# Delta rule over 32 head pairs: the inverse may cross turns, and side work on VectorE is queued behind the recurrence's last result

## The chip, the cores and the metric

The kernel runs on one core of one Trainium2 chip. The metric is the device time of one execution in microseconds (us); times of several runs are given by their median. Five engines work side by side, each through its own queue: TensorE (PE: matrix products), VectorE (DVE), ScalarE (ACT), GpSimd (POOL) and SyncE (SP, which here only starts transfers).

## The reference

A decoder layer in three parts, all in float32: a gated delta rule, a quantised cross attention, and an attention block with a mixture of experts. The change is in the first part. For 4 sequences of 512 tokens and 16 heads of width 128 it computes, token after token,

```
q, k, v = causal convolution (4 taps) and SiLU of x @ W.T
q, k    = each divided by its norm
S_t     = g_t * S_(t-1) + k_t (beta_t * (v_t - g_t * S_(t-1)^T k_t))^T
o_t     = S_t^T q_t
out     = (o * rsqrt(mean(o * o) + eps) * norm_w * silu(x @ Wg.T)) @ Wo.T
```

S is a 128 x 128 state for each head. The mean runs over all 16 heads of a token.

## The kernel before

The recurrence is done in chunks of 128 tokens, 4 for each sequence. Inside a chunk the tokens depend on each other through a triangular matrix (`at`, from the products of the keys); its inverse turns the chunk into a few matrix products. From chunk to chunk goes only the state.

The work is cut into 32 pairs: two heads of one sequence (`HG = 2`, 8 pairs a sequence, 4 sequences). For each pair there are these steps, all written as Python generators that stop at each `yield`:

- `stage1(m)` (L530): convolutions of k and q, norms, decay factors, the triangular matrices. POOL computes powers for the norms there (L566 to L570, tiles `rk`, `ee`, `ke`, `nr`), once VectorE has clamped the sums (`ss`, L565). `at` goes to memory and comes back as 32 x 32 blocks (`iA`, L641).
- `stage2_inverse(m)` (L644): the inverse of the diagonal 32 x 32 blocks by elimination, 31 rows of two operations (L654 and L655, tiles `iW` and `iT`), each on the result of the row before. Even pairs do this on VectorE, odd pairs on POOL. Then the result is written to memory (`t_d`, L658), a transposed copy too (L659, L660), and both are read back in the layout of the matmuls (`T`, L663, and `X`, L665).
- `stage2_values(m)` (L670): convolutions of v and of the gate.
- `stage3(m)` (L700): four steps that extend the block inverse to 128 x 128 (its first matmuls, L714, read `T`), and then the recurrence, chunk by chunk: L766 multiplies keys and state, VectorE makes `r` of it (L768), L775 applies the inverse, ScalarE copies the result `u` (L777), L785 makes the addition to the state, VectorE the new `state` (L790), and L793 and L795 the output `po`. At the end VectorE reads `po` in `og` (L807) and in the squares (L811).
- `output(m)` (L821): the product with Wo (L840), added up over the 8 pairs in `xa` (L845). After a sequence's last pair the rms factor follows: `rsqrt` (L118 to L123, a power on POOL, tile `a_rs`) and L858.

In turn m (the loop at L938) `stage3(m)` is the main line. After each of its steps one round of the side work is traced: `output(m-1)`, `stage1(m+2)` (two steps a round), `stage2_values(m+1)`, `stage2_inverse(m+1)` (two steps a round) and, once a sequence, the `prologue` of the next sequence. What is left when `stage3` has ended is run out at the turn's end.

This program order is not the order on the engines. A scheduler takes for each engine the work that it expects to be ready, with the program order as priority, and may move an operation far ahead. `tc.issue_after(ins)` limits that: what is traced in its block on the engine of `ins` may not stand ahead of `ins` in that engine's queue (order only, no wait for the result). Before the change it is used for POOL alone: odd pairs' rows and the gate's products stand behind the latest norms (`norms_[-1]`, L653 and L798).

Of the kernel before, what the change touches and what calls it, by code (L numbers as in the profile page):

```python
# [33 lines left out]
ALU = mybir.AluOpType  # L34
# [13 lines left out]
VD = H1 * P  # L48
# [50 lines left out]
def decoder(ctx: ExitStack, tc: tile.TileContext, a: dict, out: bass.AP):  # L99
    nc = tc.nc  # L100
# [7 lines left out]
    mhalf = const.tile([P, 64], F32, name="mhalf")  # L108
# [9 lines left out]
    def rsqrt(dst, src, pool, add=0.0, mul=1.0):  # L118

        n = src.shape[1]  # L120
        t = pool.tile([P, 64], F32, name="rsq")
        nc.vector.tensor_scalar(t[:, :n], src, mul, add, ALU.mult, ALU.add)
        nc.gpsimd.tensor_tensor(dst, t[:, :n], mhalf[:, :n], ALU.pow)  # L123

    def layernorm(dst, src, pool):

# [42 lines left out]
    def idle(n):  # L169
        for _ in range(n):  # L170
            yield
# [154 lines left out]
    with ExitStack() as st:  # L326
# [4 lines left out]
        small = st.enter_context(tc.tile_pool(name="a_small", bufs=4))  # L331
# [198 lines left out]
        def stage1(m):  # L530
# [11 lines left out]
            ss = small.tile([P, HG * TB], F32, name="ss", bufs=2)  # L542
            for p in range(HG):
                t = live.tile([P, S], F32, name="kT")
# [3 lines left out]
            xnT, beta, gam, ngam, gend, gall = seqs[b]  # L548
            gb = rows(0)
            load_weights(m + 1, 1)  # L550
            for p in range(HG):
# [3 lines left out]
                t = s1.tile([P, TB, P], F32, name="ktok")  # L555
# [6 lines left out]
            rk, ee, ke = (small.tile([P, HG * TB], F32, name=n, bufs=2) for n in ("rk", "ee", "ke"))  # L562
            nr = small.tile([P, HG * TB], F32, name="nr", bufs=4)
# [3 lines left out]
            nc.gpsimd.tensor_tensor(ee, rk, rk, ALU.mult)  # L567
            nc.gpsimd.tensor_tensor(ee, ee, flat(beta), ALU.mult)
            nc.gpsimd.tensor_tensor(ke, ee, flat(gend), ALU.mult)
            norms_.append(nc.gpsimd.tensor_tensor(nr, ss, rk, ALU.mult).ins)  # L570
            em = []
            for p in range(HG):

# [5 lines left out]
            for p in range(HG):  # L579
                scale(em[p], em[p], ee, p)  # L580
                pk = p_b.tile([P, TB, P], F32, name="pb")
# [12 lines left out]
            for p in range(HG):  # L594
# [5 lines left out]
                t = w2.tile([P, S], F32, name="cv", bufs=5)  # L600
# [3 lines left out]
                pq = p_b.tile([P, TB, P], F32, name="pb")  # L604
# [3 lines left out]
                t = live.tile([P, TB, P], F32, name="pt", bufs=6)  # L608
# [16 lines left out]
            for p in range(HG):  # L625
                t = live.tile([P, TB, P], F32, name="kdec", bufs=4)
# [4 lines left out]
            nc.gpsimd.tensor_tensor(rq, rq, mhalf[:, 0 : HG * TB], ALU.pow)  # L631
            keys[m] = (kT, kd_, qg, pt, nr, rq)

        inverses, norms_ = {}, []

        def load_blocks(m, ats):

# [6 lines left out]
        def stage2_inverse(m):  # L644

            nb = HG * TB * 4
            A, T, W, ats = inverses.pop(m)
            eng = nc.vector if m % 2 == 0 else nc.gpsimd
            for i in range(31):
                n, w = 31 - i, i + 1  # L650
                u = W[:, : n * w].rearrange("p (a b) -> p a b", a=n)

                with tc.issue_after(norms_[-1]) if m % 2 and m > 1 else ExitStack():  # L653
                    eng.tensor_tensor(u, A[:, i, i + 1 :].unsqueeze(2).to_broadcast([nb, n, w]), T[:, i, :w].unsqueeze(1).to_broadcast([nb, n, w]), ALU.mult)  # L654
                    eng.tensor_tensor(T[:, i + 1 :, :w], T[:, i + 1 :, :w], u, ALU.add)  # L655
                yield
            dT, dX = inv_d[m % 2]
            nc.sync.dma_start(blocks(dT), T)  # L658
            eng.tensor_copy(A, T.rearrange("p t j -> p j t"))  # L659
            nc.sync.dma_start(blocks(dX), A)  # L660
            yield
            t = w2.tile([P, HG * TB, P], F32, name="T", bufs=1)
            nc.sync.dma_start(t, squares(dT))  # L663
            x = w2.tile([P, HG * TB, P], F32, name="X", bufs=2)
            nc.sync.dma_start(x, squares(dX))  # L665
            Ts, Xs = ([v[:, p * TB : (p + 1) * TB, :] for p in range(HG)] for v in (t, x))
            inverses[m] = (Ts, Xs, ats)
            yield

        def stage2_values(m):  # L670

# [28 lines left out]
        def stage3(m):  # L700
# [56 lines left out]
            for c in range(TB):  # L757
                cs = slice(c * P, (c + 1) * P)
                rs = []
                for p in range(HG):  # L760
                    h = hg * HG + p
                    if c == 0:
                        rs.append(v_[p][:, 0, :])
                        continue
                    pk = p_s.tile([P, P], F32, name="ps")
                    nc.tensor.matmul(pk, kT[p][:, cs], st_[p], start=True, stop=True)  # L766
                    r = small.tile([P, P], F32, name="r", bufs=3)
                    nc.vector.scalar_tensor_tensor(r, pk, ngam[:, h, c : c + 1], v_[p][:, c, :], ALU.mult, ALU.add)  # L768
                    rs.append(r)
                if c:  # L770
                    yield
                us = []
                for p in range(HG):
                    pu = p_s.tile([P, P], F32, name="ps")
                    nc.tensor.matmul(pu, Xs[p][:, c, :], rs[p], start=True, stop=True)  # L775
                    u = small.tile([P, P], F32, name="u", bufs=4)
                    nc.scalar.copy(u, pu)  # L777
                    us.append(u)
                yield
                nst = list(st_)  # L780
                for p in range(HG):
                    h = hg * HG + p
                    if c < TB - 1:
                        pn = p_s.tile([P, P], F32, name="ps")
                        nc.tensor.matmul(pn, kd_[p][:, c, :], us[p], start=True, stop=True)  # L785
                        s_ = small.tile([P, P], F32, name="state", bufs=4)
                        if c == 0:
                            nc.scalar.copy(s_, pn)
                        else:
                            nc.vector.scalar_tensor_tensor(s_, st_[p], gall[:, h, c : c + 1], pn, ALU.mult, ALU.add)  # L790
                        nst[p] = s_
                for p in range(HG):
                    nc.tensor.matmul(po[p][:, c, :], us[p], pt[p][:, c, :], start=True, stop=c == 0)  # L793
                    if c > 0:
                        nc.tensor.matmul(po[p][:, c, :], st_[p], qg[p][:, cs], start=False, stop=True)  # L795
                st_ = nst
                if 0 < c <= HG:
                    with tc.issue_after(norms_[-1]):  # L798
                        nc.gpsimd.tensor_tensor(gs[c - 1], gs[c - 1], rb[c - 1], ALU.mult)
                yield  # L800

# [19 lines left out]
        def output(m):  # L821


            b, hg = divmod(m, NHG)
            og = outs.pop(m)
            wot = w2.tile([P, HG, D], F32, name="wot", bufs=2)
            nc.sync.dma_start(wot, a["a_wo"][hg])
            xs = []

            def load(c):  # L830
                xs.append(w2.tile([P, D], F32, name="x_in", bufs=2))
                nc.sync.dma_start(xs[c], x_t[:, b * TB + c, :])

            if hg == NHG - 1:
                load(0)
                load(1)
            for c in range(TB):
                pw = p_b.tile([P, D], F32, name="pb")
                for p in range(HG):
                    nc.tensor.matmul(pw, og[p][:, c * P : (c + 1) * P], wot[:, p, :], start=p == 0, stop=p == HG - 1)  # L840
                if hg == 0:
                    xa[c] = w2.tile([P, D], F32, name="xa", bufs=4)
                    nc.vector.tensor_copy(xa[c], pw)
                else:
                    nc.vector.tensor_tensor(xa[c], pw, xa[c], ALU.add)  # L845
                yield
            if hg == NHG - 1:
                yield from idle(4)
                pq = p_b.tile([P, TB], F32, name="pb")
                for c in range(TB):  # L850
                    nc.tensor.matmul(pq[:, c : c + 1], acc[b][:, c * P : (c + 1) * P], ones1, start=True, stop=True)
                rs = small.tile([P, TB], F32, name="a_rs")
                yield
                rsqrt(rs, pq, small, add=1e-6, mul=1.0 / VD)
                yield
                for c in range(TB):
                    xr = xa[c]
                    nc.vector.scalar_tensor_tensor(xr, xr, rs[:, c : c + 1], xs[c], ALU.mult, ALU.add)  # L858
                    if c + 2 < TB:
                        load(c + 2)  # L860

                    (nc.gpsimd if m == NP - 1 else nc.sync).dma_start(x1d[b * TB + c], xr)
                    yield
# [72 lines left out]
        run(itertools.islice(pair0, 3 * HG + 1))  # L936
        run(turns((stage2_inverse(0), 2), (chain(pair0, turns((stage1(1), 2), (stage2_values(0), 1))), 1), (prepare(), 1)))
        for m in range(NP):  # L938
            rest = []
            if m == NP - 2:  # L940
                first.close()
                x_keep = top.enter_context(tc.tile_pool(name="x_keep", bufs=1, side="right", reuse_waits="tile"))
# [16 lines left out]
                rest.append((stage1(m + 2), 2))  # L959
            if m + 1 < NP:  # L960
                rest.append((stage2_values(m + 1), 1))
                rest.append((stage2_inverse(m + 1), 2))
            if (m + 4) % NHG == 0 and (m + 4) // NHG < B:
                rest.append((prologue((m + 4) // NHG), 1))
            rest = turns(*rest)
            for _ in stage3(m):
                next(rest, None)
            run(rest)
        run(turns((output(NP - 1), 1), (cross(1), 2)))

# [572 lines left out]
```

## Time and profile before

| what | value |
|---|---|
| median of 3 runs | 3871.29 us (3865.89 to 3873.21) |
| the profiled execution | 3873.35 us, its span on the core 3871.6 us |
| TensorE busy | 3445.1 us, 89% of the span |
| VectorE busy | 2243.0 us, 58% |
| ScalarE busy | 1568.5 us, 41% |
| POOL busy | 1379.5 us, 36% |
| mean granted TensorE clock | 0.942 |

The delta rule takes the first 56% of the span: the first L714 starts at 150.9 us, the last at 2114.4 us. The other two parts follow.

```profile
PE   5898999789987989897889789999999999898897
...
L655 POOL TENSOR_TENSOR iT<-iT,iW 32x31 f32<-32x31 f32 (+15 forms) x496 | 275.8, 556 | 38.9
L654 POOL TENSOR_TENSOR iW<-iA,iT 32x31 f32<-32x31 f32 (+15 forms) x496 | 268.6, 541 | 41.1 <-DMA iA<-at_d 2.4
...
L655 DVE TENSOR_TENSOR iT<-iT,iW 32x31 f32<-32x31 f32 (+15 forms) x496 | 211.9, 427 | 10.3
...
L654 DVE TENSOR_TENSOR iW<-iA,iT 32x31 f32<-32x31 f32 (+15 forms) x496 | 204.2, 412 | 10.7
...
L775 PE MATMUL ps<-r,X 128*128 128x128 f32 x384 | 81.4, 311 | 139.0 <-DVE r L768 138.4
```

The first line is TensorE's busy share in 40 equal slices of the span, in tenths. A group's line reads: line, engine, operation, output and inputs, count | busy us in all, mean ns of one | idle us of the engine just ahead of it, and what ended most of that. TensorE is busy nearly everywhere; where it is not, the question is what the next instruction in its queue waited for.

### The profile page before, as it was taken

The page shows a single profiled execution, that of the slowest core. Times are in us where ns is not written, and L with a number is a line of the kernel's source. Part 1 is how long each engine was busy: PE and PEld are TensorE (multiplying, and loading weights), DVE is VectorE, ACT ScalarE, POOL GpSimd, SP SyncE. Part 2 cuts the span into 40 slices and gives each one's busy share as a digit, 9 for nine tenths or more (in the row PEclk, how much of TensorE's full clock was granted, in tenths as well). Part 3 has the DMA queues.
Part 4 walks back from the last instruction along what each step waited for, and adds up shares of the span by engine and source line. Part 5 has one row for each costly group of instructions (what it writes and reads, how often), then busy time and mean ns, then how long its engine had stood idle before and what let it go on. Part 6 is the DMA issues. An engine that isn't in the chain of part 4 may idle for free. (4 is left out here: it accounts for less than half of the span.)

```text
span 3871.6 us, 48770 instructions
## 1 busy us (share of the span) xinstructions
PE 3445.1 (89%) x16466; PEld 1947.6 (50%) x16466; DVE 2243.0 (58%) x4923; ACT 1568.5 (41%) x4382; POOL 1379.5 (36%) x1941
## 2 busy tenths in 40 slices
PE   5898999789987989897889789999999999898897
PEld 3455555445554545454545445555555555454443
DVE  5477766666675667656764556655665565554111
ACT  3444444335443435343433334444444444343121
POOL 1425553455355444543455222113212221211442
PEclk8899999899998999998999899999999999999898
DMA  5333334333333334334333155445544444456444
GB/s 158 109 101 101 100 88 119 109 99 100 114 99 107 97 108 113 95 89 130 96 96 111 56 176 161 143 146 158 161 134 139 144 139 143 139 173 204 82 82 92
DMA packets 391880, 465.56 MB, mean 120 GB/s; under 512 B 128451, under 2 KB 242115, under 8 KB 391440
## 3 DMA queue, kind: packets, MB, share of 16 engines
q1 hardware_dynamic: 380080, 438.03, 38.0%
q0 software_dynamic: 10112, 21.58, 3.1%
q8 instruction: 132, 2.16, 0.2%
q10 hardware_dynamic: 1440, 2.84, 0.2%
q14 instruction: 116, 0.95, 0.1%
HBM read 401.76 MB, written 64.81 MB: 121 GB/s over the span
## 5 line engine op out<-in xcount | busy, mean ns | idle before, releaser
L511 PE MATMUL pb<-xnT,w 128*128 128x512 f32 x2048 | 972.5, 615 | 0.0
L511 PEld LDWEIGHTS pb<-xnT,w 128*128 128x128 f32 x2048 | 385.2, 198 | 429.9 <-issue 412.0
L522 DVE SCALAR_TENSOR_TENSOR cv<-pb,pp,cv 128x511 f32<-128x511 f32 (+2 forms) x576 | 427.1, 741 | 230.5 <-ACT cv L519 209.8
L1085 PE MATMUL pb<-c_q,hT 128*128 128x512 f32 x768 | 357.1, 603 | 10.6 <-DMA c_q<-in_c_wq_dram 6.0
L655 POOL TENSOR_TENSOR iT<-iT,iW 32x31 f32<-32x31 f32 (+15 forms) x496 | 275.8, 556 | 38.9
L654 POOL TENSOR_TENSOR iW<-iA,iT 32x31 f32<-32x31 f32 (+15 forms) x496 | 268.6, 541 | 41.1 <-DMA iA<-at_d 2.4
L519 ACT ACTIVATE cv<-pb,pp 128x512 f32<-128x512 f32 x192 | 148.2, 772 | 263.5 <-PE pb L511 263.5
L840 PE MATMUL pb<-wot,og 128*128 128x512 f32 x512 | 251.1, 613 | 0.0
L1191 PE MATMUL pw<-c_o,oT 128*128 128x512 f32 x512 | 240.7, 600 | 2.9 <-DVE oT L1183 2.9
L1085 PEld LDWEIGHTS pb<-c_q,hT 128*128 128x128 f32 x768 | 142.0, 193 | 166.3 <-issue 149.3
L655 DVE TENSOR_TENSOR iT<-iT,iW 32x31 f32<-32x31 f32 (+15 forms) x496 | 211.9, 427 | 10.3
L566 POOL TENSOR_TENSOR rk<-ss,mhalf 128x8 f32<-128x8 f32 x32 | 53.3, 1666 | 460.2 <-DVE ss L565 460.2
L1157 ACT ACTIVATE e<-pb,nm,rq 128x128 f32<-128x128 f32 (+3 forms) x256 | 157.0, 618 | 140.3 <-DVE nm L1155 108.7
L654 DVE TENSOR_TENSOR iW<-iA,iT 32x31 f32<-32x31 f32 (+15 forms) x496 | 204.2, 412 | 10.7
L775 PE MATMUL ps<-r,X 128*128 128x128 f32 x384 | 81.4, 311 | 139.0 <-DVE r L768 138.4
L274 POOL TENSOR_SCALAR x_e<-x_e 128x1024 f32<-128x1024 f32 x64 | 68.1, 1064 | 331.0 <-ACT x_e L269 241.2
L1181 PE MATMUL po<-eT,val 128*128 128x512 f32 x320 | 171.0, 628 | 6.8 <-ACT eT L1179 3.8
L598 POOL TENSOR_TENSOR qg<-qh,row 128x512 f32<-128x512 f32 x64 | 84.5, 1325 | 223.3 <-ACT qh L525 221.1
L1151 PE MATMUL pb<-kT,qT 128*128 128x256 f32 (+3 forms) x576 | 162.7, 409 | 0.8 <-ACT x_e L269 0.8
L269 ACT ACTIVATE x_e<-pb,nm 128x256 f32<-128x256 f32 x256 | 118.2, 477 | 102.4 <-DVE nm L266 102.4
L775 PEld LDWEIGHTS ps<-r,X 128*128 128x128 f32 x384 | 63.1, 204 | 171.1 <-DVE r L768 149.6
L1013 POOL TENSOR_TENSOR rope_s<-q,tab 128x128 f32<-128x128 f32 x64 | 35.2, 550 | 314.9 <-DVE q L1115 269.3
(330 smaller groups left out, 6629.1 us busy)
## 6 DMA issues: line engine op xcount, KB each, us to landing
c_o<-in_c_wo_dram SPq DMA_DIRECT2D x128, 512.0 KB, 4.2
c_q<-in_c_wq_dram SPq DMA_DIRECT2D x128, 512.0 KB, 4.6
w<-in_a_w_dram SPq DMA_DIRECT2D x124, 512.0 KB, 4.2
row<-g_d SPq DMA_DIRECT2D x64, 512.0 KB, 5.0
at_d<-at SPq DMA_DIRECT2D x64, 256.0 KB, 2.2
T<-t_d SPq DMA_DIRECT2D x32, 512.0 KB, 6.1
X<-x_d SPq DMA_DIRECT2D x32, 512.0 KB, 6.6
rrow<-r_d SPq DMA_DIRECT2D x32, 512.0 KB, 3.8
```

The costliest lines, as they stand in the source:

```text
L511: nc.tensor.matmul(pj, wt[:, kd, p * P : (p + 1) * P], xnT[:, kd, :], start=kd == 0, stop=kd == KD - 1)
L519: nc.scalar.activation(ac, pj, AF.Identity, bias=cb[:, m, h : h + 1], scale=cw[:, m, h, 3:4])
L522: nc.vector.scalar_tensor_tensor(ac[:, j:], pj[:, : S - j], cw[:, m, h, 3 - j : 4 - j], ac[:, j:], ALU.mult, ALU.add)
L654: eng.tensor_tensor(u, A[:, i, i + 1 :].unsqueeze(2).to_broadcast([nb, n, w]), T[:, i, :w].unsqueeze(1).to_broadcast([nb, n, w]), ALU.mult)
L655: eng.tensor_tensor(T[:, i + 1 :, :w], T[:, i + 1 :, :w], u, ALU.add)
L775: nc.tensor.matmul(pu, Xs[p][:, c, :], rs[p], start=True, stop=True)
L840: nc.tensor.matmul(pw, og[p][:, c * P : (c + 1) * P], wot[:, p, :], start=p == 0, stop=p == HG - 1)
L1085: nc.tensor.matmul(pj, hT[:, kd, :], w[:, kd % 2, :], start=kd == 0, stop=kd == KD - 1)
L1151: nc.tensor.matmul(ps[:, m, k * P : (k + w) * P], qT[g][:, n + m, :], kT[:, g, j : j + w, :], start=True, stop=True)
L1157: nc.scalar.activation(e[n + m][:, :nk], ps[:, m, :nk], AF.Exp, bias=nm[:, n + m : n + m + 1], scale=rq, accum_out=es[:, n + m : n + m + 1])
L1181: nc.tensor.matmul(po, val[:, g, :], eT, start=k == 0, stop=k == c)
L1191: nc.tensor.matmul(pw, oT[:, h + m, :], w[:, m, :], start=g == 0 and h + m == 0, stop=g == 3 and h + m == 3)
```

## The change

A new generator `inversions` takes the place of `stage2_inverse(m + 1)` in the side work: it first finishes the inverse of pair m+1, and then, from step 10 of the turn's 15 on, may begin that of pair m+2 and hand it over in `begun`. Every round of side work is traced behind `vital[-1]`, the latest `r` or `state` that VectorE makes for the recurrence. `norms_` becomes `factors`, to which the rms factor of a sequence's end also belongs; pair 1 is tied to it too. Four idle rounds in `output` become two and two.

```diff
-        nc.gpsimd.tensor_tensor(dst, t[:, :n], mhalf[:, :n], ALU.pow)
+        return nc.gpsimd.tensor_tensor(dst, t[:, :n], mhalf[:, :n], ALU.pow).ins
...
-            norms_.append(nc.gpsimd.tensor_tensor(nr, ss, rk, ALU.mult).ins)
+            factors.append(nc.gpsimd.tensor_tensor(nr, ss, rk, ALU.mult).ins)
...
-        inverses, norms_ = {}, []
+        inverses, begun, vital, factors = {}, {}, [], []
...
-                with tc.issue_after(norms_[-1]) if m % 2 and m > 1 else ExitStack():
+                with tc.issue_after(factors[-1]) if m % 2 else ExitStack():
...
+        def inversions(m, step, turn):
+
+            if m + 1 < NP:
+                yield from begun.pop(m + 1) if m + 1 in begun else stage2_inverse(m + 1)
+            if m + 2 < NP:
+                while turn and (turn[0] < step or m + 2 not in inverses):
+                    yield
+                begun[m + 2] = stage2_inverse(m + 2)
+                while turn:
+                    next(begun[m + 2])
+                    yield
...
-                    nc.vector.scalar_tensor_tensor(r, pk, ngam[:, h, c : c + 1], v_[p][:, c, :], ALU.mult, ALU.add)
+                    vital.append(nc.vector.scalar_tensor_tensor(r, pk, ngam[:, h, c : c + 1], v_[p][:, c, :], ALU.mult, ALU.add).ins)
...
-                            nc.vector.scalar_tensor_tensor(s_, st_[p], gall[:, h, c : c + 1], pn, ALU.mult, ALU.add)
+                            vital.append(nc.vector.scalar_tensor_tensor(s_, st_[p], gall[:, h, c : c + 1], pn, ALU.mult, ALU.add).ins)
...
-                    with tc.issue_after(norms_[-1]):
+                    with tc.issue_after(factors[-1]):
...
-                yield from idle(4)
+                yield from idle(2)
...
-                rsqrt(rs, pq, small, add=1e-6, mul=1.0 / VD)
+                factors.append(rsqrt(rs, pq, small, add=1e-6, mul=1.0 / VD))
                 yield
                 for c in range(TB):
+                    if c == 2:
+                        yield from idle(2)
...
-            rest = []
+            rest, turn = [], [0]
...
-                rest.append((stage2_inverse(m + 1), 2))
+                rest.append((inversions(m, 10, turn), 2))
...
             for _ in stage3(m):
-                next(rest, None)
+                with tc.issue_after(vital[-1]) if vital else ExitStack():
+                    next(rest, None)
+                turn[0] += 1
+            turn.clear()
             run(rest)
```

## The prediction

> **What bounds the kernel now.** First the busy table and its stretches: TensorE is busy 1762 of the 2000 us between 165 and 2165, the 32 turns of the delta rule, and nothing in the diff acts after them. So at most some 240 us of TensorE idleness is at stake. Then the waits of TensorE in that stretch (us in total, times, longest):
>
> ```profile
> PE ps L775 <- DVE r L768: 138.4, 50, 13.1
> PE pb L714 <- DMA T<-t_d: 40.4, 8, 6.2
> PE ps L766 <- DVE state L790: 15.5, 9, 7.4
> ```
>
> Two causes: the recurrence's result `r` comes late from VectorE, and a pair's inverse `T` comes late from memory. L714 is the first work of a turn. Its starts in the timeline divide the turns: odd turns take 58.0 us on average (15 of them, 1 to 29), even ones 68.2, those with a prologue (4, 12, 20) 73.2, those with a sequence's end (8, 16, 24) 78.1. Turns 14 and 15 by stretch (PE, PEld, DVE, ACT, POOL busy):
>
> ```profile
> 1044.24:1112.78 68.54, 55.02 (x298) 31.84 (x297) 48.24 (x82) 26.88 (x78) 39.25 (x56) 0.94 0.29 76
> 1112.78:1171.29 58.51, 56.38 (x297) 32.00 (x297) 35.78 (x73) 25.56 (x76) 22.16 (x33) 0.95 0.40 112
> ```
>
> TensorE has 55 to 56 us of work in either. Turn 14's timelines of PE, POOL and SP, in that order, show where the rest goes:
>
> ```profile
> 1098.02 0.80 PE L775 MATMUL ps<-r,X 128*128 128x128 f32 x2 [5.40 <-DVE r L768]
> ...
> 1106.17 0.39 PE L795 MATMUL po<-qg,state 128*128 128x128 f32 x2
> ...
> 1112.78 0.26 PE L714 MATMUL pb<-T,at 128*32 128x32 f32 x1 [6.22 <-DMA T<-t_d]
> ```
>
> ```profile
> 1069.49 1.65 POOL L566 TENSOR_TENSOR rk<-ss,mhalf 128x8 f32<-128x8 f32 x1 [18.89 <-DVE ss L565]
> ...
> 1102.80 0.30 POOL L655 TENSOR_TENSOR iT<-iT,iW 32x31 f32<-32x31 f32 x1
> ```
>
> ```profile
> 1103.12 0.31 SPq L658 DMA_DIRECT2D t_d<-iT  x1
> ...
> 1106.25 0.46 SPq L663 DMA_DIRECT2D T<-t_d  x1
> ```
>
> See in it: the odd pair's inverse runs on POOL. From `rk` (25.25 us into the turn) to the write of `t_d` are 33.6 us, from there to L714 9.7. That chain ends the turn; without the 5.4 us stall TensorE would have waited 11.6 at L714. The even pair's inverse, on VectorE, is done in the middle of the odd turn (its last row at 1137.6, needed at 1171.3), so no even turn waits for its `T`.
>
> **What the Trainium skill says.** "PSUM — Partial Sum Buffer", section Engine vs sequencer instructions: the queues of ScalarE, VectorE and GpSimd are strict FIFO and matmuls start in program order. The trace agrees: L714 has 6.22 us of idle TensorE ahead of it though the convolution behind it (L511) needs nothing of `T`. "TensorE: Matmul & The Clock Gate", section What's actually happening: after an idle window of some 3.4 us the array runs at half clock for about as long. Agreed: the first twelve L511 records of a turn take 8.02 us after the 6.22 us wait and 5.42 in turn 14, which had none. "SBUF — State Buffer", section SBUF: two separate sides: VectorE with two SBUF inputs and GpSimd exclude each other on a shared port. Agreed: the elimination's VectorE rows take 0.6 to 0.7 us beside POOL's and 0.3 to 0.4 alone.
>
> **The change, part by part.** No arithmetic is added or removed; only order.
>
> 1. *The early start.* An inverse takes 33 yields (31 rows and two), the generator is advanced twice a round, so it ends in round 17. A turn has 15 yields of stage3 (4 for the solve, 2 for chunk 0, 3 each for the others). So in round 15 it stands at row 29; `turn.clear()` comes before the rest is run out, and the begun inverse then finds `turn` empty and takes no step. Each turn thus hands nothing on. The early start never happens: worth 0.
>
> 2. *VectorE work queued behind `vital[-1]`.* Rows of the even pair were floated by the scheduler into idle time of the turn before. Now row 2k or 2k+1 may not stand ahead of the recurrence result of its round. In the built program's order, turn 15 to 16 on VectorE ends
>
> ```
> L768 r x2 (chunk 3)
> rows 24 to 29 of pair 16, between them L575 em x2
> L807 og x2, L811 cv x2
> row 30 of pair 16, L659 copy
> ```
>
> and this holds for every even pair from 2 to 30: row 30 stands behind `og`, which waits for the turn's last L795. TensorE's order still has L714 directly behind L795. So in odd turns L714 must now wait for og, cv, row 30, the write of `t_d` and the read of `T`.
>
> Odd turn, from its L714, taking turn 15's offsets (it too follows a wait, so it starts cold): `r` of chunk 1 at 28.5 as before. Rows now between the results delay `state` by 1 us and the chunk-2 `r` to 43.3; the new TensorE order puts 4 us of other matmuls there, so I count 2 us of stall where before were 1.5+0.35. Chunk-3 `r` is done at 55.5, L795 at 59. VectorE still has two scans (1.2 each), 12 row operations (6 us beside POOL, 3 alone; I take 4.4 with the gaps): og starts at 62.3, og and cv take 1.41+1.28, row 30 0.4: 65.4. SP's queue has the `rq`, `r_d` and `rrow` transfers ahead of L658; by the same trace they pass at about 66. Write to landing 2.3 (list of transfers), issue of the read to L714 6.5 (1106.25 to 1112.78): 66+2.3+0.1+6.5 = 75, against 58: +17. Floor: L795 ends at 57, og at once, 57+2.7+0.4+2.3+0.1+6.5 = 69. Ceiling, if all rows run at the shared-port price and stalls add up to 4 us: 80.
>
> Even turn: the POOL order behind `rk` is the same (1 row operation, gs, 1, gs, 40), so the stall at L775 that goes turns into a longer wait at L714. The turn now begins cold, `rk` at 27.7 (as turns 3, 7, 11 after a wait: 27.5 to 28.0): 27.7+33.6+9.7, less 0.6 because a weight load moved behind the read of `T`: 70.4, +2.2. What is late next is nothing: TensorE arrives at about 60.
>
> 3. *Sequence ends (turns 8, 16, 24).* `rsqrt` moves ahead, and POOL's rows wait for it, so L858 no longer waits 19.5 us for POOL's `a_rs`, and the stalls of 13.1 and 6.5 us go. But then POOL's chain with the extra power (0.6) ends the turn: 71 instead of 78.1.
>
> 4. *Small ones.* Pair 1 (odd) is now tied to `factors` too: turn 0 becomes 27.0+33.6+9.1 = 70 instead of 59.5. Three fewer table loads on ScalarE, hidden under TensorE. Prologue turns have 8 us more matmuls, which cover POOL's chain: 72 instead of 73.2. Turn 30 starts cold: +2.
>
> Sum: 15 odd turns x 17 = +255; 8 plain even turns (2, 6, 10, 14, 18, 22, 26, 28) x 2.2 = +18; prologue 3 x -1 = -3; ends 3 x -7 = -21; turn 0 +10; turn 30 +2: +261. The profiled execution took 3873.35 (span 3871.6), the median of the runs is 2 less: 3871+261 = 4132.
>
> **Rivals.**
>
> *The floor.* As forecast, but VectorE reaches og when L795 ends: 69 to 70.5 in odd turns, +165 to +188 in them, with the rest some 4050. For it: VectorE is busy only 36 of 58 us in turn 15. Against: some rows that stood in turn 14 are now in turn 15, and two scans stand behind the last `r`.
>
> *VectorE becomes the bound.* Odd turns of 80 and more: at least 4210. For it: 45 row operations at up to 0.65 us, and PSUM is held until VectorE has evacuated. Against: POOL works on rows in parallel only in parts of the odd turn.
>
> *The stalls go and nothing takes their place* (faster). Place: L775 in odd turns and turns 8, 16, 24. If row 30 were out before og, L714 of even turns would find its `T`, and 15 x 1.5 + 3 x 7 = 43 us would be saved: 3830. It decides from the point where row 30 and the write come some 12 us ahead of L795. If the early start also took effect for the POOL pairs, all three waits above would go: 3871-194 = 3677. Against: the order of the built program, the same in all 15 odd turns.
>
> **How the numbers follow.** Forecast (odd turns of 70.5 to 79.5) 0.82; floor 0.07; VectorE bound 0.07; nothing in their place 0.03; the two effects cancelling 0.01. A measurement of this kernel can tell about 0.2% from no change. Range: 15 x -4.5 from 4132 is about 4065, 15 x +4 with 5 more in the even turns about 4195; this leaves out little more than the two neighbours. Faster 0.03, same 0.01, slower 0.96.
>
> **What would show it.** Right: L714 waits for `T` in nearly every turn, some 15 us at the start of even turns and 9 to 11 at that of odd ones, together about 370 us; the wait of L775 for `r` falls from 138 to under 50; the copy L659 on VectorE comes behind L811; L858's wait for `a_rs` is gone; odd turns near 75, plain even ones near 70. Wrong: an even turn that begins without a wait for `T` (then row 30 was out in time), or L775's wait still above 100 us (then VectorE, not the inverse, is the bound).

## The result, and the profile after

The changed kernel takes 4069.87 us (median of 4 runs, 4068.42 to 4075.21), the kernel before 3870.56 us in the same comparison (4 runs, 3865.89 to 3873.21). The ratio is 1.0519, interval 1.0501 to 1.0537: 5.2% slower. The profiled execution took 4070.2 us, its span 4068.4 us.

The page's table of busy time and its line of TensorE by slices:

```profile
PE 3452.6 (85%) x16466; PEld 1942.1 (48%) x16466; DVE 2273.2 (56%) x4923; ACT 1572.8 (39%) x4379; POOL 1390.2 (34%) x1941
...
PE   5878787877978787887878788999999999899797
```

TensorE has the same work (3445.1 us before); its share falls, and only in the slices of the delta rule. Its mean granted clock fell from 0.942 to 0.924, but its busy time rose by only 7.5 us, so the loss is nearly all waiting, not slower matmuls. The last turn starts at 2310.8 us instead of 2114.4: the 196 us that were lost lie in the turns. TensorE's waits in that stretch, in the changed kernel (us in total, times, longest; the lines of code have moved by 12: L714 is L726, L766 is L778, L775 is L787):

```profile
PE pb L726 <- DMA T<-t_d: 325.2, 29, 15.1
PE pb L607 <- ACT qh L525: 47.9, 15, 3.2
PE ps L787 <- DVE r L780: 28.2, 16, 3.1
PE ps L778 <- DVE state L802: 10.5, 15, 0.7
```

The wait for `r`, 138 us before, has shrunk to 28; the wait for `T` has grown from 40 to 325 us, and comes in 29 turns instead of 8. One thing was late, now another is, and by more. The lengths of the turns (from one start of L714 or L726 to the next, in us):

| turns | before | predicted | after |
|---|---|---|---|
| odd, 1 to 29 (mean of 15) | 58.0 | 75 | 73.7 |
| plain even (mean of 8) | 68.2 | 70.4 | 66.7 |
| with a prologue (4, 12, 20) | 73.2 | 72 | 67.6 |
| with a sequence's end (8, 16, 24) | 78.1 | 71 | 72.9 |
| 0 | 59.5 | 70 | 62.8 |
| 30 | 34.6 | 36.6 | 36.6 |

Only the odd turns and the first and last are longer than before: 15 x 15.7 = +236, 8 x -1.5 = -12, 3 x -5.6 = -17, 3 x -5.2 = -16, and +5 for turns 0 and 30, together +196. Turns 14 and 15 by stretch (columns as before):

```profile
1138.76:1205.92 67.16, 54.27 (x296) 31.27 (x297) 37.44 (x65) 24.79 (x74) 33.84 (x52) 0.93 0.22 59
1205.92:1278.75 72.83, 56.79 (x297) 32.29 (x297) 46.40 (x88) 28.23 (x80) 26.78 (x37) 0.90 0.40 120
```

TensorE's 54 and 57 us of work are what they were. VectorE did 82 instructions in turn 14 and 73 in turn 15; now it does 65 and 88: the rows of the even pair's inverse have moved from the even turn into the odd one. The end of turn 15 shows what they do there. VectorE's timeline, then SP's, then TensorE's:

```profile
1261.22 0.59 DVE L780 SCALAR_TENSOR_TENSOR r<-ps,ngam,vn 128x128 f32<-128x128 f32 x2
...
1267.17 0.21 DVE L655 TENSOR_TENSOR iT<-iT,iW 32x60 f32<-32x60 f32 x1
1267.31 1.39 DVE L819 SCALAR_TENSOR_TENSOR og<-po,pp,gs 128x512 f32<-128x512 f32 x2
1268.63 1.27 DVE L823 TENSOR_TENSOR cv<-po,rrow 128x512 f32<-128x512 f32 x2
1269.83 0.17 DVE L654 TENSOR_TENSOR iW<-iA,iT 32x31 f32<-32x31 f32 x1
1270.03 0.18 DVE L655 TENSOR_TENSOR iT<-iT,iW 32x31 f32<-32x31 f32 x1
```

```profile
1269.93 0.32 SPq L764 DMA_DIRECT2D rrow<-r_d  x1
1270.34 0.38 SPq L658 DMA_DIRECT2D t_d<-iT  x1
...
1274.63 0.39 SPq L663 DMA_DIRECT2D T<-t_d  x1
```

```profile
1266.29 0.39 PE L807 MATMUL po<-qg,state 128*128 128x128 f32 x2
...
1278.75 0.26 PE L726 MATMUL pb<-T,at 128*32 128x32 f32 x1 [12.08 <-DMA T<-t_d]
```

The last `r` of the turn is done at 1261.8. Between it and `og` stand twelve row operations and two scans; row 30, the last, stands behind `og` and `cv`. The result is written at 1270.3, read back from 1274.6, and TensorE, which has had nothing since 1266.7, goes on at 1278.75. Row 30 stands behind `og` and `cv` in 14 of the 15 odd turns. In turn 29 it stands ahead of them, yet it is done no earlier (65.7 us into the turn, 64.3 in turn 15), and the turn is no shorter (72.8 us).

### The profile page after: what moved, and what is told of

Its sections match the earlier page's. It is cut to its first block, busy times and chain, and to the rows that moved or that the text cites. A ratio compares the mean times of both kernels' runs of the same rounds, so it can differ in the third digit from the quotient of the medians.

```text
span 4068.4 us, 48733 instructions
## 1 busy us (share of the span) xinstructions
PE 3452.6 (85%) x16466; PEld 1942.1 (48%) x16466; DVE 2273.2 (56%) x4923; ACT 1572.8 (39%) x4379; POOL 1390.2 (34%) x1941
## 5 line engine op out<-in xcount | busy, mean ns | idle before, releaser
L511 PE MATMUL pb<-xnT,w 128*128 128x512 f32 x2048 | 1027.7, 641 | 0.0
L522 DVE SCALAR_TENSOR_TENSOR cv<-pb,pp,cv 128x509 f32<-128x509 f32 (+2 forms) x576 | 423.3, 742 | 481.7 <-ACT cv L519 475.0
L511 PEld LDWEIGHTS pb<-xnT,w 128*128 128x128 f32 x2048 | 398.5, 207 | 423.8 <-issue 397.5
L654 POOL TENSOR_TENSOR iW<-iA,iT 32x31 f32<-32x31 f32 (+15 forms) x496 | 259.3, 523 | 154.6 <-issue 69.5
L655 POOL TENSOR_TENSOR iT<-iT,iW 32x31 f32<-32x31 f32 (+15 forms) x496 | 285.8, 576 | 38.9
L726 PE MATMUL pb<-T,at 128*32 128x32 f32 x512 | 19.8, 236 | 325.2 <-DMA T<-t_d 325.2
L655 DVE TENSOR_TENSOR iT<-iT,iW 32x31 f32<-32x31 f32 (+15 forms) x496 | 229.9, 464 | 11.5
L654 DVE TENSOR_TENSOR iW<-iA,iT 32x31 f32<-32x31 f32 (+15 forms) x496 | 215.2, 434 | 9.2
L726 PEld LDWEIGHTS pb<-T,at 128*32 128x32 f32 x512 | 15.7, 146 | 331.7 <-DMA T<-t_d 328.8
L1465 PE MATMUL pb<-w_gu,eT 128*128 x312 | 142.2, 599 | 3.5 <-issue 3.5
```

The costliest lines, as they stand in the source:

```text
L511: nc.tensor.matmul(pj, wt[:, kd, p * P : (p + 1) * P], xnT[:, kd, :], start=kd == 0, stop=kd == KD - 1)
L522: nc.vector.scalar_tensor_tensor(ac[:, j:], pj[:, : S - j], cw[:, m, h, 3 - j : 4 - j], ac[:, j:], ALU.mult, ALU.add)
L1465: nc.tensor.matmul(pg, hT[:, kd, :], w_gu[:, bass.ds(e, 1), kd, :, :], start=kd == 0, stop=kd == KD - 1)
```

## The experiments

Each kernel is the changed one with the edit shown, unless said otherwise. Each was run beside the kernel before on the same chip, and the ratio is to that; the kernel before took 3874.91 to 3878.18 us there. The theory at the start: the place of VectorE's rows in its queue is the whole loss; the generator that may begin an inverse early does nothing. The rival: the queueing of the other side work behind the recurrence costs too.

**The rows alone are freed.** The inverse is traced outside the block; everything else stays behind `vital[-1]`.

```diff
-                rest.append((inversions(m, 10, turn), 2))
+                rows_.append((inversions(m, 10, turn), 2))
...
                 with tc.issue_after(vital[-1]) if vital else ExitStack():
                     next(rest, None)
+                next(rows_, None)
```

> The changed kernel with one thing undone: the rows of the inverse are traced outside the guard, all other side work stays behind the recurrence's last result. In the built order the even pair's last row and copy then stand in the middle of the odd turn again. My theory (the time is lost because the even pair's inverse ends behind og): the wait of the odd turn's end goes, odd turns fall from 73.6 to about 58 us, even turns stay near 67 since POOL still has 42 row operations behind rk: 4070 - 15 x 15.6 = some 3835. Rival (queueing convolutions and the other side work behind the recurrence is what costs, by ScalarE and TensorE waiting for late VectorE results): little changes, above 4000.

The rows also become a stream of their own here, traced behind each round and, at the turn's end, ahead of the rest.

Measured: 3833.53 us, ratio 0.9887 (0.9853 to 0.992). Odd turns 57.1, plain even ones 65.7. The wait for `T` falls to a fifth. No row is left at the turn's end: VectorE goes from the scans to `og` and waits there for TensorE. TensorE's waits in the turns of this kernel, and then VectorE's timeline at the end of turn 15:

```profile
PE pb L726 <- DMA T<-t_d: 64.5, 13, 8.8
PE pb L607 <- ACT qh L525: 63.2, 15, 6.3
PE ps L787 <- DVE r L780: 51.8, 31, 3.8
```

```profile
1146.25 2.65 DVE L575 TENSOR_TENSOR_SCAN em<-row,tab_a 128x512 f32<-128x512 f32 x2
1151.18 1.41 DVE L819 SCALAR_TENSOR_TENSOR og<-po,pp,gs 128x512 f32<-128x512 f32 x2 [2.28 <-PE po L807]
```

So the place of the rows costs 4070 - 3834 = 236 us (some 245 by the two ratios), more than the whole loss. The rival falls: with the other work still queued behind the recurrence the kernel is faster than the one before. That the stream of their own does it is ruled out by the next experiment, where the rows are free without it and the odd turns are as short as before.

**No queueing behind `vital[-1]` at all.** The line with `issue_after` in the loop is taken out; the generator, `factors` and the idle rounds stay.

```diff
-                with tc.issue_after(vital[-1]) if vital else ExitStack():
-                    next(rest, None)
+                next(rest, None)
```

> The changed kernel without the guard: nothing is queued behind the recurrence's last result; the generator, the earlier rms factor and the tie of POOL's rows to it stay. My theory: the generator does nothing, so this is the kernel before but for turns 8, 16 and 24 (from 78 to about 73 us) and the start: 3871 - 15 = about 3856, and VectorE's r still late (L775 waits some 100 us for it). Rival (the generator or the tie to the rms factor costs part of the loss): above 3900.

Measured: 3862.54 us, ratio 0.9965 (0.9955 to 0.9975). Odd and plain even turns are the ones of before (58.2 and 68.2). The three ends are shorter (70.7 to 71.6 for 78.1), some 3 x 7 = 21 us by the earlier rms factor, and turn 0 is 4.8 us longer, since pair 1 is now tied to the norms. Together that is -16 us, and the times differ by 15: the generator adds nothing that could be seen. Of the wait for `r`, 138.4 before, two thirds stay, and the wait for `T` is what it was (40.4):

```profile
PE ps L787 <- DVE r L780: 93.3, 44, 5.4
PE pb L726 <- DMA T<-t_d: 42.9, 9, 6.1
```

Against this kernel the queueing of everything but the rows, in the first experiment, gains 3863 - 3834 = 29 us.

**The inverse one round in three steps instead of two.** With 33 yields it is then done in round 11, and the early start can happen.

```diff
-                rest.append((inversions(m, 10, turn), 2))
+                rest.append((inversions(m, 10, turn), 3))
```

> The changed kernel with one number changed: the inverse takes three steps a round in place of two, so that it ends in round 11 and the next pair's really begins in the same turn. In the built order POOL has 2 row operations left behind rk in even turns (42 in the changed kernel), and VectorE's copy stands ahead of the last chunk's r in odd turns. My theory (both ends of a turn wait for an inverse that the rate makes late): both waits for T go, all turns near 58 us, prologue turns near 65: 4070 - 15 x 15.6 - 8 x 9 - 3 x 3 - 3 x 14 = some 3710. Rival (VectorE or the late side work is the bound once the waits are gone): turns of 63 or more, above 3830.

Measured: 3848.01 us, ratio 0.9929 (0.9903 to 0.9954), far from what was expected. Hardly a wait of L726 for `T` is left (2.5 us in all), but the cost has changed its place, as turn 10 shows. Timelines of VectorE, POOL, ScalarE and TensorE, in that order:

```profile
792.78 0.17 DVE L565 TENSOR_SCALAR ss<-ss 128x8 f32<-128x8 f32 x1 [1.79 <-ACT pb L559]
```

```profile
803.41 0.29 POOL L655 TENSOR_TENSOR iT<-iT,iW 32x60 f32<-32x60 f32 x1
...
803.78 1.65 POOL L566 TENSOR_TENSOR rk<-ss,mhalf 128x8 f32<-128x8 f32 x1
```

```profile
807.70 2.45 ACT L397 ACTIVATE em<-em,ee 128x128 f32<-128x128 f32 x8 [14.64 <-POOL ee L568]
```

```profile
811.02 1.22 PE L797 MATMUL ps<-u,kdec 128*128 128x128 f32 x4 [9.97 <-ACT u L789]
```

`ss` is ready at 792.95, but `rk` starts only at 803.78: of the pair's 62 row operations 60 now stand ahead of the norms in POOL's queue, where there were 20 ahead in the changed kernel, and the last 20 of them had yet to end when `ss` came. ScalarE waits 14.64 us for `ee`, and `u`, which the recurrence needs, stands behind that in ScalarE's queue. So the early start does take place, and makes the norms 10.8 us late.

**Three steps, no early start.**

```diff
-                rest.append((inversions(m, 10, turn), 2))
+                rest.append((stage2_inverse(m + 1), 3))
```

> The changed kernel with three steps a round and without the hand-over to the next turn: each inverse begins and ends in its own turn. POOL has 32 row operations behind rk (42, or 2 with the hand-over); VectorE's last row stands just ahead of the last chunk's r. My theory: the POOL chain of the even turn is 10 operations or 7 us shorter, so even turns near 60 us, odd ones near 62: about 3810, which is some 100 us above the run with the hand-over; so the early start, where it takes effect, is worth about that. Rival (the rate alone does it and the hand-over is worth nothing): equal to that run within 20 us.

Measured: 3760.61 us, ratio 0.9699 (0.9667 to 0.9732). The order of the two was expected the other way: beginning early for all pairs loses 87 us against not beginning early. Even turns 56.3, odd ones 62.4. Its waits in the turns:

```profile
PE ps L787 <- DVE r L780: 74.1, 31, 4.2
...
PE pb L726 <- DMA T<-t_d: 13.9, 9, 3.1
```

**The kernel before with three steps** (no other part of the change):

```diff
-                rest.append((stage2_inverse(m + 1), 2))
+                rest.append((stage2_inverse(m + 1), 3))
```

> The kernel before with one number changed, three steps of the inverse a round in place of two: no guard, no hand-over. POOL has 32 operations behind rk in place of 42. My theory: even turns lose their wait for T but keep the late r (5.4 us of L775 on VectorE's floated rows), so they fall from 68 to about 62, the rest is as before: some 3820; the guard is worth the 60 us from there to the run with guard and three steps (3761). Rival (the guard is worth nothing, the rate alone made that run): 3770 or less.

Measured: 3788.9 us, ratio 0.9777 (0.9761 to 0.9794). The number 3 alone brings 86 us: no turn begins with a wait for `T` any more, while the late `r` stays.

```profile
PE ps L775 <- DVE r L768: 118.6, 47, 7.7
```

The changed kernel's other parts (queueing, earlier factor) bring some 28 more, not the 60 expected. From this kernel to the one with three steps and no early start, time moves about: odd turns 57.0 to 62.4, plain even ones 63.5 to 56.3, ends 71.1 to 59.8. In the plain turns that is 15 x 5.4 = +81 and 8 x -7.2 = -58 us, so they lose 23 us there; the gain comes from the ends, the prologue turns and turn 0, some 51 us together.

**The early start for even pairs only** (their rows run on VectorE), with three steps:

```diff
-            if m + 2 < NP:
+            if m + 2 < NP and m % 2 == 0:
```

> Three steps a round, and only the even pairs (VectorE) are begun a turn ahead; POOL's pairs begin in their own turn. The run with the hand-over for all left POOL's powers for the norms behind 20 more row operations, so that ScalarE, and with it u, came up to 10 us late. If that is the reason why it fell short: POOL's order is now that of the run without hand-over (32 operations behind rk), VectorE's that of the run with it, so even turns stay near 57 us and odd ones fall from 62.4 to about 59: some 3710. If the hand-over on VectorE itself does the harm (rows behind the last r delay what follows): no better than 3760.

Measured: 3761.72 us, ratio 0.9704 (0.9685 to 0.9722), no different from none at all. Even turns 56.1, odd ones 60.1, but prologue turns take 70 to 75 where they took 66 to 68 without the early start; why is not shown.

**Three steps, rows freed, no early start:** the edit of the first experiment with `(stage2_inverse(m + 1), 3)` in `rows_`.

> Three steps a round, no hand-over, and the rows traced outside the guard, so that the scheduler may float VectorE's rows into the turn before. Theory (the guard keeps the rows between the results of the odd turn, which is what its 74 us of waits of L787 for r are): odd turns 57 as in the run with free rows, even turns 57 to 58: some 3710. Rival (floated rows delay r in the even turn as in the kernel before): even turns above 60, near 3760 again.

Measured: 3773.79 us, ratio 0.9733 (0.9713 to 0.9753). Odd turns 57.2 as expected, but plain even ones 59.8, prologue turns 77, ends 67.4. With three steps the rows lose nothing in all by being queued: freed, they are not faster (3773.79 us to 3760.61, with intervals that overlap). So the queueing does its harm at two steps, where the last rows fall behind the turn's last `r`.

**A later start of the next inverse,** so that POOL takes fewer rows ahead of the norms: three steps, step 13 instead of 10.

```diff
-                rest.append((inversions(m, 10, turn), 2))
+                rest.append((inversions(m, 13, turn), 3))
```

> Three steps a round and the hand-over for all pairs, but from step 13 on in place of 10. In the built order POOL has 20 operations behind rk (2 with step 10, 32 without hand-over). If POOL's rows ahead of rk are what step 10 paid for, the 20 that are done from the turn's start to ss (25 us) cost nothing: even turns near 56, odd near 60, some 3725. If any hand-over on POOL delays the norms: like step 10, above 3800.

Measured: 3753.07 us, ratio 0.9675 (0.9654 to 0.9697). Even turns 54.7, odd ones 60.3, ends 57.2; prologue turns take 79. There a third thing on POOL comes late, the power for the layer norm of the next sequence. Timelines of VectorE and POOL in such a turn, turn 12:

```profile
877.44 0.55 DVE L137 TENSOR_SCALAR x_in<-x_in,ln_mv,ln_rs 128x512 f32<-128x512 f32 x1 [13.89 <-POOL ln_rs L123]
```

```profile
876.16 0.61 POOL L655 TENSOR_TENSOR iT<-iT,iW 32x231 f32<-32x231 f32 x1
876.85 0.55 POOL L123 TENSOR_TENSOR ln_rs<-rsq,mhalf 128x1 f32<-128x1 f32 x1
```

The power `ln_rs` stands behind POOL's rows.

**The same, with no early start ahead of a prologue turn.**

```diff
-            if m + 2 < NP:
+            if m + 2 < NP and (m + 5) % NHG:
...
-                rest.append((inversions(m, 10, turn), 2))
+                rest.append((inversions(m, 13, turn), 3))
```

The condition leaves out turns 3, 11 and 19, which come ahead of a prologue turn, and turn 27.

> Three steps a round, hand-over from step 13 on, but none in the turns before a prologue (3, 11, 19), where the prologue's powers stood behind POOL's floated rows and VectorE waited 14 us for them. If that is what makes those three turns 79 us long: they fall to the 68 of the run without hand-over, the rest stays at 54.7 and 60.2: 3753 - 3 x 11 = some 3720. If the length comes from elsewhere in the prologue: no change from 3753.

Measured: 3727.85 us, ratio 0.9616 (0.96 to 0.9632): 3.8% faster than the kernel before, and the fastest of all. Prologue turns take 69. TensorE's waits in its turns, and turns 14 and 15 by stretch:

```profile
PE ps L787 <- DVE r L780: 57.6, 31, 4.2
PE pb L554 <- ACT kT L525: 20.2, 15, 1.5
PE ps L778 <- DVE state L802: 17.8, 16, 2.1
```

```profile
983.93:1038.59 54.66, 52.72 (x297) 30.59 (x297) 30.09 (x57) 26.53 (x77) 33.07 (x51) 1.00 0.45 134
1038.59:1099.47 60.88, 56.28 (x297) 33.01 (x296) 45.89 (x98) 26.11 (x77) 28.34 (x42) 0.94 0.31 89
```

The wait for `T` is gone from the list. TensorE is idle for 2 us of the even turn and 4.6 of the odd one.

**Only row 30 ahead of `og`.** Two steps and the queueing as in the change, but three yields fewer, so that the inverse ends in the last round.

```diff
-                yield
+                if i > 2:
+                    yield
```

> The changed kernel, two steps a round and with the guard, but the inverse's first four rows share one yield, so that it takes 30 yields in place of 33 and its last row and copy are traced within the turn: in the built order they stand just ahead of og, not behind og and the squares, and POOL has 36 operations behind rk in place of 42. The theory says a turn's length follows the place of that last row: T some 6 us earlier in odd turns (about 67 in place of 73.7), and POOL's chain 4 us shorter in even ones (about 63): some 3925. If the loss comes from the guard's effect on the rest of the side work, it stays above 4030.

Measured: 3997.43 us, ratio 1.0312 (1.0292 to 1.0332). Odd turns 71.3 (67 expected), plain even ones 63.4 (63 expected). The ends of turn 15 on VectorE and SP in this kernel:

```profile
1222.02 0.60 DVE L781 SCALAR_TENSOR_TENSOR r<-ps,ngam,vn 128x128 f32<-128x128 f32 x2
...
1227.95 0.18 DVE L655 TENSOR_TENSOR iT<-iT,iW 32x31 f32<-32x31 f32 x1
1228.16 1.02 DVE L660 COPY iA<-iT 32x1024 f32<-32x1024 f32 x1
1229.11 1.39 DVE L820 SCALAR_TENSOR_TENSOR og<-po,pp,gs 128x512 f32<-128x512 f32 x2
```

```profile
1227.55 1.11 SPq L622 DMA_DIRECT2D rq<-sr  x2
1228.72 0.58 SPq L538 DMA_DIRECT2D row<-g_d  x1
1229.34 0.43 SPq L659 DMA_DIRECT2D t_d<-iT  x1
```

Row 30 is done at 1228.1 and stands ahead of `og`, but eight row operations still stand behind the last `r`, and then SP issues the write 1.2 us after the row is done, behind the issues of `rq` and `row`. From the last `r` to the write are 6.7 us instead of 8.5. On the mean of the 15 odd turns row 30 is done 4.0 us earlier than in the changed kernel (61.5 us into the turn for 65.5), but the write is issued only 3.1 us earlier, with other transfers ahead of it as in the lines above, and the read of `T`, which waits for the write to land, only 2.3 us earlier. That is part of why 71.3 came and not 67. `og` and `cv` were not the main part of the lateness (4.0 of 15.7 us); that the rows run until after the last `r` is.

## Why the prediction was right, and which terms were off

The direction and the path of the loss were right; its size was 199 us where 261 had been forecast. 4070 us lies only 5 us above the lower end of the stated range, 4065: of the six kinds of turns four were put too high and only one, the sequence ends, too low.

*Step 1, the early start is worth nothing.* Right: without the queueing the time is that of before but for the ends and turn 0, so the generator neither helps nor harms. Only with three steps does it hand anything on, and then it harms through POOL's queue.

*Step 2, VectorE's rows behind the recurrence.* The mechanism was right in its order and place: the copy (L659) comes behind `cv` in 14 of the 15 odd turns, L726 waits in nearly every turn (325 us in all for the 370 forecast), the wait for `r` is under 50 us. That the place of the rows is the loss is shown by the first two experiments together. That the last row stands behind `og` and `cv`, which the prediction stressed, is the smaller part of it, as the run with 30 yields shows: without that its odd turns are only 2.4 us shorter. The sizes along turn 15, from its start at 1205.92:

| | predicted | measured |
|---|---|---|
| last `r` done | 55.5 | 55.9 |
| `og` starts | 62.3 | 61.4 |
| row 30 done | 65.4 | 64.3 |
| write of `t_d` issued | 66 | 64.4 |
| L726 | 75 | 72.8 |

Three terms were off. The 12 row operations were priced at 4.4 us, between the price alone and that beside POOL; with the two scans they took 5.5 us, as 3 would have given. And the end, from write to matmul, was 8.4 us for 8.9, which is right by luck, for two errors nearly cancel: the read alone needed 4.1 us for the 6.5 taken from turn 14 of before, while the read was issued 4.3 us after the write instead of 2.4. SP waits there for the write to land. In 11 of the 15 odd turns the 512 KB read of `rrow` (L764) was issued 0.4 to 0.8 us ahead of the write, as in the lines of SP above, and the read followed the write after 4.0 to 5.1 us; in the four turns without it, after 2.3 to 3.2. The prediction named that transfer as being ahead in the queue, but gave it no price at the landing.

*The even turns* were put at +2.2 and came out at -1.5, the largest single miss (8 x -3.7 = -30 us). Turn 14 after, by the terms of the sum: `rk` at 26.7 for 27.7, from there to the write 32.9 for 33.6, from the write to L726 7.6 for 9.1; on the mean of the eight turns 27.0, 32.9 and 6.9. The first is the cold start, which was set too high. What the Trainium skill says in "TensorE: Matmul & The Clock Gate", section What's actually happening, was the ground for it, and the trace agrees that a start after a wait is slower: the first twelve L511 records of a turn take 5.42 us without a wait. After the eight waits of before, 4.3 to 6.2 us long, they take 6.7 to 8.0 (mean 7.5); after 26 waits of the changed kernel, 9.9 to 15.1 us long, 6.6 to 8.1 (mean 7.25). So the loss spread from 1.2 to 2.7 us and did not grow with the wait; the 8.02 that had been read in turn 15 was the largest of its eight. The third, and the largest, is the 512 KB load of weights that moved behind the read of `T`, for which 0.6 us were taken off. In SP's timeline of turn 14, the changed kernel:

```profile
1200.89 0.39 SPq L663 DMA_DIRECT2D T<-t_d  x1
1201.38 0.62 SPq L502 DMA_DIRECT2D w<-in_a_w_dram  x1
```

From this issue to L726 are 5.0 us; before, with the load issued 0.62 us ahead of the read, 6.5. The same holds throughout: over the eight turns of before that wait for `T`, all with such a load ahead, 5.7 to 6.6 us; over the 28 of after with none ahead, 3.8 to 5.3. On the mean of the eight plain even turns it is 4.3 us for 6.3. If the move of the load is the cause, it was worth about 2 us at the read besides the 0.6; no run moved the load alone.

*Step 3, the ends.* 71 predicted, 72.9 measured. The VectorE wait in L872 for `a_rs` falls from 58.5 us in all to 1.3, as said, and POOL's chain ends the turn. That chain was priced too low: in turn 8 it takes 36.5 us from `rk` to the write for 33.6 + 0.6, since the power takes 1.0 us and a product of POOL (L598, 1.3 us) now stands among the rows.

*Step 4.* Prologue turns were held at 72 by their additional matmuls; they take 67.6, because the POOL chain ends them too. In turn 4: `rk` at 27.9, 31.4 to the write, 7.8 to L726, together 67.1. Turn 0 was given a chain from 27.0; `rk` is at 21.0 there, and the turn takes 62.8 (21.0+32.9+8.9).

The sum of these against the forecast: 15 x -1.3 (odd), 8 x -3.7 (plain even), 3 x -4.4 (prologue), 3 x +1.9 (ends) and -7 (turn 0) are some -63, from 4132 to 4069.

*The rivals.* Neither floor nor ceiling came: odd turns lie at 72.7 to 76.2. VectorE is not the bound: in the fastest run its turn 15 has 98 instructions, more than the 88 here, and takes 60.9 us. The faster rival, a `T` that is out in time, was priced at 3830; with the rows freed the kernel takes 3834. That is in part luck: some 20 us of its gain come from the plain even turns (8 x -2.5), which the rival put at nothing. What it named as the deciding point, row 30 some 12 us ahead of the last L795, fits: with three steps a round and no early start row 30 is done 12.6 us ahead of it on the mean of the odd turns, with 30 yields and two steps 0.5 us behind it. The 3677 for an early start that works was wrong: it left out that POOL's rows would then stand ahead of the norms.

*Not foreseen:* L607 now waits 47.9 us for `qh`, 3.2 us in each of the 15 odd turns, some 41 us into the turn. The prediction had counted 2 us of stall there, at `r`. ScalarE's line in turn 15 shows what `qh` waits for:

```profile
1246.51 0.63 ACT L525 ACTIVATE qh<-cv 128x512 f32<-128x512 f32 x1 [1.02 <-DVE cv L522]
```

It waits for a convolution (L522) whose last pieces stand behind `state` and behind a row in VectorE's queue. With the rows freed the wait is 63.2 us at two steps a round and 51.1 at three, but it lies in the even turns; without the queueing it is 15.5 us, in the prologue turns alone; with queued rows at three steps it is 4.8. What moves it so stays open.

## What to carry to other kernels

Where work is tied behind a result in an engine's queue, ask which of its own last pieces somebody waits for: here a chain of 31 dependent rows, two yields a round, was still unfinished when the turn's 15 rounds were over, so its end came behind the turn's last result, and its reader paid for everything after that. Try the rate at which such a chain is traced before moving where it starts: one digit brought 86 us to the kernel before. And count what an earlier start puts ahead of whom on its own engine: 20 row operations that had yet to run ahead of one small power made a chain on two other engines late.

## What the runs showed of the hardware that was not expected

Where a load of 512 KB was issued 0.6 us ahead of the read of `T`, that read came some 2 us later: 5.7 to 6.6 us from issue to the matmul that waits, in nine cases, against 3.8 to 4.5 in 15 cases with no such load near. Where the load was issued 0.5 to 1.3 us behind, it was later by up to 1 (3.9 to 5.3, 13 cases). The changed kernel has one read of the first kind, at the start of turn 1, and it took 5.9 us. The small write of `t_d` (128 KB) shows the same: the read that waits for its landing is issued 4.0 to 5.1 us after it in the 11 odd turns of the changed kernel with a 512 KB read of `rrow` issued 0.4 to 0.8 us ahead of it, and 2.3 to 3.2 us after it in the four others. That the transfer ahead is the cause is argued from these cases; no run moved such a transfer alone.

The loss of a cold start did not grow with the wait: the first twelve matmul records took 6.7 to 8.0 us after waits of 4.3 to 6.2 us, and 6.6 to 8.1 after waits of 9.9 to 15.1 us, against 5.42 without a wait.
